# Queries one pair ahead, shared products in the last step, and a pair's rows turned a step later

## The chip, the cores and the metric

The kernel runs on one core of a Trainium2 chip. The metric is the device time of one execution in microseconds; for the kernel before, the median of three runs.

## The reference, cut to what matters

A decoder layer in fp32 over 1024 tokens (16 sequences of 64) of width 512. Each of three parts is added to its own input: an attention over the batch, a cross attention with 8 key heads of 4 query heads each, and a layer of experts. The change lies at the seam of the last two.

```
q = rmsnorm(layernorm(x) @ Wq.T);  p = softmax(q k.T / sqrt(128) + mask)
x = x + layernorm(x) + (p v) @ Wo.T          # 8 heads, summed over heads
h = layernorm(x)
scores = sigmoid(h @ gate.T) + bias;  top 4 of 16 experts, weights normed
x = x + h + sum_e w_e * Wd_e(silu(Wg_e h) * (Wu_e h)) + Sd(silu(Sg h) * (Su h))
```

## The kernel before, in words

The 1024 tokens are eight tiles of 128, taken in four **pairs** u = 0 to 3. The cross attention is a list of **steps** (g, u), head g = 0 to 7 and pair u. `cross` walks heads 4 and 5 in order, then heads 6 and 7 in turn, so that its last eight steps are (6,0), (7,0), (6,1), (7,1), ... (6,3), (7,3). A pair is complete once head 7 has run for it.

A step issues these pieces:

- `softmaxed` (L490): for both tiles, `normed_queries` scales the queries (L479), turns them (L482) and copies them to `qt` (L484, ScalarE); 64-column score products (L499); then on VectorE scale and mask (L504), maximum (L509), subtraction (L510), the exponential on ScalarE (L511), sum (L513), reciprocal (L514), product (L515).
- `queries` (L446): the query projection of a pair to come, seven products of two matmuls each (a Strassen-like scheme; `seven`, L254), evacuated on VectorE (L458 to L462) and squared on ScalarE (L466); their root (L442) is taken for one or more pairs at once.
- `projected` (L545): the output projection of the step before, again 14 matmuls, added into `acc` and `more` (L552, L557 to L559).
- `attended` (L518): the probabilities are turned (L521) and copied to `pt` (L525, ScalarE), multiplied by the values (L531), copied to `at` (L537, ScalarE), and combined to `sat` and `at` by four VectorE operations (L228 to L231) for heads 6 and 7.

After a pair is complete, `summed` (L571) combines the parts of its projection, and `normed_pair` (L622) takes the layer norm, writes the rows `xm` (L632), turns them with TensorE (L635), copies them to `xnT` (L636), and sends them to memory on SP's queue (L637). `routed_pair` (L689) multiplies them by the gate (L694), ranks the experts by comparing all with all (L710 to L714), counts (L722, L723), and leaves slots and weights; for pairs 0 to 2 `entered` (L776) scatters them to tables in memory with eight indirect DMAs from GpSimd. After the last pair, the tables are read on SP's queue (L793), added on GpSimd (L796 to L799), and joined with what the last pair adds by 8 matmuls (L771). Some small products make the lists of rows and experts for each block; `steer` (L898, L899) holds the expert of each block. Then SP issues the loads of expert weights (L926, three DMAs of 512 KB for a block that starts a new expert), and GpSimd gathers rows (L935). A block is turned (L943), multiplied by gate and up weights (L951) and by down weights (L971), and scattered into the output (L976).

Between the last pair's routing and the experts TensorE has the shared expert: `shared_half(0)` and `shared_half(1)`, each 16 matmuls of 512 columns (L825), a silu (L831), a product on VectorE (L832, `sz`), 8 matmuls (L839) and their addition to `acc` (L844).

What decides the order: the tile framework orders each engine's instructions when the program is built, by its own estimate of when each could start; each engine then runs its list in that order and waits where an operand is not there. PSUM is dealt out in three rings of banks: `mm` (3), `tr` (2) and `sc` (3).

Of the kernel before, what the change touches and what calls it, by code (L numbers as in the profile page):

```python
# [23 lines left out]
F32 = mybir.dt.float32  # L24
I32 = mybir.dt.int32
AF = mybir.ActivationFunctionType
ALU = mybir.AluOpType
# [21 lines left out]
def decoder_layer(  # L49
# [521 lines left out]
    def summed(u):  # L571
        x_sum, u3, c1, c2 = sums_of(u)
        V.tensor_add(x_sum[:, 1], x_sum[:, 0], x_sum[:, 1])
# [8 lines left out]

    def cross(steps):
        for g, u in steps:
# [4 lines left out]
            pr = softmaxed(g, u)  # L589
            if g < KVH - 2:  # L590
                queries(*divmod(NT // 2 * g + u + 3, NT // 2))
            elif g == KVH - 2:
                queries(g + 1, u)
            if (g, u) == (KVH - 3, NT // 2 - 1):
                queries(g + 1, u)
            if late:
                projected(*late.pop())
            late.append((g, u, *attended(g, u, pr)))
            if g == KVH - 2 and u > 0:
                summed(u - 1)  # L600
# [21 lines left out]
    def normed_pair(u):  # L622
# [5 lines left out]
        rs = inverse_root(mv[:, :, 1], [P, 2], 1.0)  # L628
        for j in range(2):
# [7 lines left out]
            nc.sync.dma_start(rows_d[i * P : (i + 1) * P, :], xm)  # L637
# [51 lines left out]
    def routed_pair(u):  # L689
# [15 lines left out]
        for j in range(2):  # L705
            other = sc[:, j, :].unsqueeze(1).to_broadcast([P, E, E])
            own = sc[:, j, :].unsqueeze(2).to_broadcast([P, E, E])
            gt = route.tile([P, E, E], F32, tag="gt", name="gt", bufs=1)
            eq = route.tile([P, E, E], F32, tag="eq", name="eq", bufs=1)
            V.tensor_tensor(gt, other, own, ALU.is_gt)  # L710
            V.tensor_tensor(eq, other, own, ALU.is_equal)
            V.tensor_mul(eq, eq, before_sb)
            V.tensor_add(gt, gt, eq)
            V.tensor_reduce(rank[:, j, :], gt, AX.X, ALU.add)  # L714
# [132 lines left out]
    def shared_half(th, queue):  # L847
        z = shared_hidden(th)
        for j in range(4):
            shared_out(th, z, j, queue)  # L850
# [228 lines left out]
```

## Time and profile before

| | us |
|---|---|
| median of 3 runs (1032.02 to 1035.42) | 1033.96 |
| the profiled execution | 1035.67 |
| its span, first to last instruction | 1033.7 |
| TensorE busy in the span | 979.8 |
| VectorE, ScalarE, GpSimd busy | 542.0, 435.3, 319.8 |
| first product of an expert block (L951) starts at | 800.5 |

The profile is of one execution. In its stretches, the steps (6,0) to (7,3) run from about 609 us to 748 us, the shared expert beside the last routing to 799 us, and the expert blocks to the end. Where rows of TensorE are shown, one fp32 matmul is two records of the profile, so "x8" is four matmuls. "PE" is TensorE, "DVE" VectorE, "ACT" ScalarE, "POOL" GpSimd, "SPq" the queue of SyncE. A bracket at the end of a row gives the idle time before it and what ended it. ScalarE loads a table of functions (`ACT_TABLE_LOAD`) when it goes from one kind of function to another (square root, exponential, silu).

### The profile page before, as it was taken

How to read it: one execution, taken by the hardware profiler on the slowest of the kernel's cores; microseconds unless marked ns; L12 is line 12 of the kernel's file. 1: busy time of each engine (PE TensorE's matmuls, PEld its weight loads, DVE VectorE, ACT ScalarE, POOL GpSimd, SP SyncE). 2: the span in 40 equal slices, each digit the busy share in tenths (PEclk: the TensorE clock that was granted, in tenths of full speed). 3: DMA queues.
4: the chain of work that ended last, by engine and by line, in shares of the span. 5: the costliest groups of instructions: out<-in, count | busy, mean ns of one | idle time of the engine just before them, and what ended most of it. 6: DMA issues, size and time to landing. Idle time of an engine off the chain costs nothing.

```text
span 1033.7 us, 13575 instructions
## 1 busy us (share of the span) xinstructions
PE 979.8 (95%) x4560; PEld 686.7 (66%) x4560; DVE 542.0 (52%) x1156; ACT 435.3 (42%) x1151; POOL 319.8 (31%) x318
## 2 busy tenths in 40 slices
PE   9999998999999999999999998988899999999974
PEld 3455556788888888887888887876654454545431
DVE  4566667574855747557557577768674111111100
ACT  2366663764545544535455554343220222222220
POOL 2131111512523417134252350033044343434332
PEclk9999999999999999999999999999799999999997
DMA  9120024200202002021020110001035856764643
GB/s 250 48 92 21 11 53 102 82 1 1 82 2 79 3 1 82 1 92 41 1 83 1 42 41 1 21 22 42 1 92 220 309 126 142 155 144 79 158 113 55
DMA packets 28362, 74.70 MB, mean 72 GB/s; under 512 B 4544, under 2 KB 8944, under 8 KB 26240
## 3 DMA queue, kind: packets, MB, share of 16 engines
q1 hardware_dynamic: 17728, 51.39, 15.0%
q0 software_dynamic: 10272, 22.13, 10.8%
q8 instruction: 38, 0.62, 0.3%
q14 instruction: 36, 0.29, 0.1%
q10 hardware_dynamic: 288, 0.26, 0.1%
HBM read 98.64 MB, written 14.97 MB: 110 GB/s over the span
## 4 chain that ended last, share of the span: by engine, by line
PE 76%; DVE 9%; ACT 5%; DMA 4%; issue 3%; POOL 1%; SPq 0%; ACTq 0%; POOLq 0%; DVEq 0%
PE mm L254 26%; PE sc L951 11%; PE sc L499 6%; PE mm L971 5%; PE sc L254 4%; PE sc L531 3%; PE mm L270 3%; PE tr L482 3%; PE sc L825 2%; PE mm L297 2%; DMA out_dram<-y,idx 2%; PE tr L297 2%; ACT square L466 2%; PE tr L943 1%; PE mm L839 1%
## 5 line engine op out<-in xcount | busy, mean ns | idle before, releaser
L951 PE MATMUL sc<-w,xt 128*128 128x512 f32 x288 | 131.4, 600 | 1.2 <-ACT xt L945 1.1
L466 ACT ACTIVATE square<-qraw 128x128 f32<-128x128 f32 x256 | 79.2, 309 | 74.7 <-DVE qraw L460 37.0
L976 POOL DMA_INDIRECT out_dram<-y,idx x36 | 56.8, 1578 | 120.5 <-DMA out_dram<-y,idx 82.6
L951 PEld LDWEIGHTS sc<-w,xt 128*128 128x128 f32 x288 | 52.6, 193 | 55.1 <-issue 53.2
L228 POOL TENSOR_TENSOR sat<-at 128x256 f32<-128x256 f32 x24 | 19.8, 823 | 209.9 <-ACT at L537 209.8
L956 DVE TENSOR_TENSOR z<-sc,z 128x256 f32<-128x256 f32 x36 | 15.3, 424 | 131.1 <-ACT z L955 131.1
L254 PE MATMUL mm<-wo_sb,at 128*128 128x256 f32 x256 | 70.5, 403 | 5.4 <-ACT at L537 5.4
L499 PEld LDWEIGHTS sc<-kT,qt 128*128 128x128 f32 x512 | 61.7, 191 | 18.0 <-ACT qt L484 9.9
L254 PE MATMUL mm<-wq_t,xns 128*128 128x256 f32 x256 | 70.5, 385 | 2.9 <-POOL wq_t L236 1.8
L971 PE MATMUL mm<-w,zt 128*128 128x512 f32 x144 | 68.2, 596 | 2.6 <-DVE zt L964 2.1
L254 PE MATMUL mm<-wq_sb,xnT 128*128 128x256 f32 x256 | 70.4, 381 | 0.0
L499 PE MATMUL sc<-kT,qt 128*128 128x64 f32 x512 | 69.1, 280 | 0.1
L254 PE MATMUL mm<-wo_t,sat 128*128 128x256 f32 x256 | 67.4, 383 | 0.6 <-DVE sat L229 0.6
L504 DVE SCALAR_TENSOR_TENSOR prob<-sc,mask_sb 128x512 f32<-128x512 f32 x32 | 22.0, 688 | 80.4 <-PE sc L499 80.4
L479 DVE TENSOR_TENSOR qraw<-qraw,rs 128x512 f32<-128x512 f32 x64 | 63.5, 1029 | 0.6
L782 POOL DMA_INDIRECT table_d<-entry_sb,at_slot x24 | 26.0, 1085 | 112.3 <-DVE at_slot L749 105.9
L254 PEld LDWEIGHTS mm<-wo_sb,at 128*128 128x128 f32 x256 | 50.9, 202 | 14.4 <-ACT at L537 7.2
L955 ACT ACTIVATE z<-sc 128x256 f32<-128x256 f32 x36 | 13.8, 384 | 108.4 <-PE sc L951 105.5
L254 PEld LDWEIGHTS mm<-wo_t,sat 128*128 128x128 f32 x256 | 48.6, 193 | 7.4 <-POOL wo_t L237 0.7
L254 PEld LDWEIGHTS mm<-wq_t,xns 128*128 128x128 f32 x256 | 46.8, 190 | 8.7 <-POOL wq_t L236 2.0
L971 PEld LDWEIGHTS mm<-w,zt 128*128 128x128 f32 x144 | 26.9, 190 | 35.8 <-issue 32.0
L484 ACT ACTIVATE qt<-tr,qw_sb 128x512 f32<-128x512 f32 x64 | 43.6, 689 | 16.5 <-PE tr L482 16.5
(272 smaller groups left out, 2039.4 us busy)
## 6 DMA issues: line engine op xcount, KB each, us to landing
w<-in_wg_dram SPq DMA_DIRECT2D x38, 512.0 KB
w<-in_wu_dram SPq DMA_DIRECT2D x38, 512.0 KB
w<-in_wd_dram SPq DMA_DIRECT2D x38, 512.0 KB
wq_sb<-in_wq_dram SPq DMA_DIRECT2D x8, 1024.0 KB
wo_sb<-in_wo_dram SPq DMA_DIRECT2D x8, 1024.0 KB
xs<-in_x_dram SPq DMA_DIRECT2D x8, 256.0 KB
wv_sb<-in_wv_dram SPq DMA_DIRECT2D x2, 1024.0 KB
ct<-in_ctxt_dram SPq DMA_DIRECT2D x8, 256.0 KB
```

The source lines that it names most:

```text
L254: T.matmul(dst, left[:, k, :], right[:, k, :], start=k == 0, stop=k == 1)
L270: T.matmul(kp, ctx_tiles[i][:, d, :], wk_sb[:, d, h * 512 : (h + 1) * 512], start=(d == 0), stop=(d == DC - 1),)
L297: T.matmul(vp, ctx_tiles[i][:, d, :], wv_sb[:, d, h * 512 : (h + 1) * 512], start=(d == 0), stop=(d == DC - 1),)
L466: S.activation(square, raw[:, h, :], AF.Square, accum_out=q_ss[g][:, 2 * u + j, h : h + 1])
L479: V.tensor_mul(raw, raw, q_rs[g, i // 2][:, i % 2, :].unsqueeze(2).to_broadcast([P, GRP, HD]))
L482: T.transpose(tp[:, j * P : (j + 1) * P], raw[:, j, :], ident)
L484: S.activation(qt.rearrange("p b h q -> p h b q"), tp.rearrange("p (h b q) -> p h b q", h=GRP, b=2), AF.Copy, scale=qw_sb,)
L499: T.matmul(sp[:, at : at + C], qt[:, b, 2 * hp : 2 * hp + 2, :], kT[g // 4][:, g % 4, k0 : k0 + C], start=True, stop=True,)
L531: T.matmul(pv[b][:, j * 256 : (j + 1) * 256], v[g // 4][rows, 2 * u + j, g % 4 * HD : (g % 4 + 1) * HD], pt[rows, j, :], start=True, stop= ...
L951: T.matmul(hp, xt[:, d, :], w1_tiles[buffer(j)][:, :, d, :], start=(d == 0), stop=(d == DC - 1))
L971: T.matmul(op, zt[:, c, :], w2_tiles[buffer(j)][:, c, :], start=(c == 0), stop=(c == FI // P - 1))
L976: G.indirect_dma_start(out, bass.IndirectOffsetOnAxis(idx[:, b : b + 1], axis=0), y, None, bounds_check=NT * P - 1, oob_is_err=False, comp ...
```

## The change

Five edits, all around the last eight steps.

1. Head 7's queries are issued in other steps: those of pair 0 in (6,0), and those of pair u+1 in (7,u). Before, (6,u) issued those of pair u.
2. A complete pair is combined and normed in head 7's next step, behind that step's softmax: `summed` now takes a multiplier `mark`, which is computed from the finished probabilities and is always 1. `normed_pair` writes its rows by ScalarE (scale and bias) in place of VectorE, sends them to memory, and returns them.
3. The turn of those rows and the copy to `xnT` are a function of their own, `pair_turned`, called a step later, in (6,2), (6,3) and, for pair 2, in (7,3); the routing follows at the end of the same step. For pairs 0 to 2 the turn uses the `mm` ring.
4. The ranking compares both tiles of a pair in one set of operations; the two counting products of each tile change places.
5. The first eight shared matmuls (with their silu and product) are issued in (7,3), in the `mm` ring.

```diff
-    def summed(u):
+    def summed(u, one=1.0):
         x_sum, u3, c1, c2 = sums_of(u)
-        V.tensor_add(x_sum[:, 1], x_sum[:, 0], x_sum[:, 1])
+        V.scalar_tensor_tensor(x_sum[:, 1], x_sum[:, 0], one, x_sum[:, 1], ALU.mult, ALU.add)
...
+    routed = {(KVH - 2, 2): 0, (KVH - 2, 3): 1, (KVH - 1, 3): 2}
+    rows = {}
...
             pr = softmaxed(g, u)
+            if g == KVH - 1 and u > 0:
+                mark = small.tile([P, 1], F32, tag="mark", name="mark", bufs=1)
+                V.tensor_tensor(mark, pr[:, 0, 0:1], pr[:, 0, 0:1], ALU.is_equal)
+                summed(u - 1, mark)
+                rows[u - 1] = normed_pair(u - 1)
             if g < KVH - 2:
                 queries(*divmod(NT // 2 * g + u + 3, NT // 2))
-            elif g == KVH - 2:
+            if (g, u) in ((KVH - 3, NT // 2 - 1), (KVH - 2, 0)):
                 queries(g + 1, u)
-            if (g, u) == (KVH - 3, NT // 2 - 1):
-                queries(g + 1, u)
+            pair = routed.get((g, u))
             if late:
                 projected(*late.pop())
+            if pair is not None and g == KVH - 2:
+                pair_turned(pair)
+            if g == KVH - 1:
+                if u + 1 < NT // 2:
+                    queries(g, u + 1)
+                else:
+                    shared_hidden(0, 0, mm_bank)
             late.append((g, u, *attended(g, u, pr)))
-            if g == KVH - 2 and u > 0:
-                summed(u - 1)
-                normed_pair(u - 1)
-                if u > 1:
-                    entered(u - 2, 1)
-            if g == KVH - 1 and u > 0:
-                routed_pair(u - 1)
-                entered(u - 1, 0)
+            if pair is not None:
+                if g == KVH - 1:
+                    pair_turned(pair)
+                routed_pair(pair)
+                if pair > 0:
+                    entered(pair - 1, 1)
+                entered(pair, 0)
...
-            V.tensor_scalar(xm, acc[:, i, :], mv[:, j, 0:1], rs[:, j : j + 1], ALU.subtract, ALU.mult)
-            tp = tr_bank()
+            S.activation(xm, acc[:, i, :], AF.Identity, bias=off[:, j : j + 1], scale=rs[:, j : j + 1])
+            nc.sync.dma_start(rows_d[i * P : (i + 1) * P, :], xm)
+            xms.append(xm)
+        return xms
+
+    def pair_turned(u):
+        for j, xm in enumerate(rows.pop(u)):
+            i = 2 * u + j
+            tp = mm_bank() if u < NT // 2 - 1 else tr_bank()
             for d in range(DC):
                 T.transpose(tp[:, d * P : (d + 1) * P], xm[:, d * P : (d + 1) * P], ident)
             S.copy(xnT[:, :, i * P : (i + 1) * P], tp.rearrange("p (d t) -> p d t", d=DC))
-            nc.sync.dma_start(rows_d[i * P : (i + 1) * P, :], xm)
...
-        for j in range(2):
-            other = sc[:, j, :].unsqueeze(1).to_broadcast([P, E, E])
...
+        other = sc.unsqueeze(2).to_broadcast([P, 2, E, E])
+        own = sc.unsqueeze(3).to_broadcast([P, 2, E, E])
...
+        V.tensor_tensor(gt, other, own, ALU.is_gt)
+        V.tensor_tensor(eq, other, own, ALU.is_equal)
+        V.tensor_mul(eq, eq, before_sb.unsqueeze(1).to_broadcast([P, 2, E, E]))
+        V.tensor_add(gt, gt, eq)
+        V.tensor_reduce(rank, gt, AX.X, ALU.add)
...
-            T.matmul(pp[:, j, :], ones_sb, taken[:, i, :], start=True, stop=False)
-            T.matmul(pp[:, j, :], tri_sb, sel[:, j, :], start=False, stop=True)
+            T.matmul(pp[:, j, :], tri_sb, sel[:, j, :], start=True, stop=False)
+            T.matmul(pp[:, j, :], ones_sb, taken[:, i, :], start=False, stop=True)
...
     def shared_half(th, queue):
-        z = shared_hidden(th)
+        for ic in range(th == 0, FI // P):
+            shared_hidden(th, ic, sc_bank)
...
     projected(*late.pop())
     summed(NT // 2 - 1)
-    normed_pair(NT // 2 - 1)
+    rows[NT // 2 - 1] = normed_pair(NT // 2 - 1)
+    pair_turned(NT // 2 - 1)
```

`shared_hidden` now does one of its two halves a call, with the banks given to it. In the order of the built program, the row writes of the last pair stand between the reads of the tables on SP's queue, with the first of the four output rows of `shared_half(0)` among them; before, all eight reads came first. In the last step the product of the shared half (L856 of the changed file, as L832 here) stands on VectorE between the subtraction (L510) and the sum (L513) of the last softmax.

More of the change, by code (lines that the diff above doesn't have):

```diff
@@ L628, in normed_pair @@
         rs = inverse_root(mv[:, :, 1], [P, 2], 1.0)
+        off = small.tile([P, 2], F32, tag="off", name="off", bufs=1)
+        V.scalar_tensor_tensor(off, mv[:, :, 0], -1.0, rs, ALU.mult, ALU.mult)
+        xms = []
         for j in range(2):
@@ L704, in routed_pair @@
         rank = route.tile([P, 2, E], F32, tag="rank", name="rank", bufs=2)
-        for j in range(2):
-            other = sc[:, j, :].unsqueeze(1).to_broadcast([P, E, E])
[L707 to L714, printed above, removed]
+        other = sc.unsqueeze(2).to_broadcast([P, 2, E, E])
+        own = sc.unsqueeze(3).to_broadcast([P, 2, E, E])
+        gt = route.tile([P, 2, E, E], F32, tag="gt", name="gt", bufs=1)
+        eq = route.tile([P, 2, E, E], F32, tag="eq", name="eq", bufs=1)
+        V.tensor_tensor(gt, other, own, ALU.is_gt)
[3 more added lines that the diff above has]
+        V.tensor_reduce(rank, gt, AX.X, ALU.add)
         sel = route.tile([P, 2, E], F32, tag="sel", name="sel", bufs=2)
@@ L816, in load_shared, with shared_hidden @@
         shared_w[part + 1] = sw
-    def shared_hidden(th):
-        z = shared.tile([P, FI // P, 512], F32, tag="sz", name="sz", bufs=1)
+    shared_z = {}
+    def shared_hidden(th, ic, new_bank):
+        if ic == 0:
+            shared_z[th] = shared.tile([P, FI // P, 512], F32, tag="sz", name="sz", bufs=1)
         sw1 = shared_w[1]
-        for ic in range(FI // P):
-            ps = [sc_bank() for _ in range(2)]
-            for s in range(2):
-                for d in range(DC):
-                    T.matmul(
-                        ps[s], sw1[:, s, d, ic * P : (ic + 1) * P],
-                        xnT[:, d, th * 512 : (th + 1) * 512],
-                        start=(d == 0), stop=(d == DC - 1),
-                    )
-            si = shared.tile([P, 512], F32, tag="ssi", name="ssi", bufs=2)
-            S.activation(si, ps[0], AF.Silu)
-            V.tensor_mul(z[:, ic, :], ps[1], si)
-        return z
+        ps = [new_bank() for _ in range(2)]
+        for s in range(2):
+            for d in range(DC):
+                T.matmul(
+                    ps[s], sw1[:, s, d, ic * P : (ic + 1) * P],
+                    xnT[:, d, th * 512 : (th + 1) * 512],
+                    start=(d == 0), stop=(d == DC - 1),
+                )
+        si = shared.tile([P, 512], F32, tag="ssi", name="ssi", bufs=1)
+        S.activation(si, ps[0], AF.Silu)
+        V.tensor_mul(shared_z[th][:, ic, :], ps[1], si)
     def shared_out(th, z, j, queue):
@@ L847, in shared_half @@
     def shared_half(th, queue):
-        z = shared_hidden(th)
+        for ic in range(th == 0, FI // P):
+            shared_hidden(th, ic, sc_bank)
         for j in range(4):
-            shared_out(th, z, j, queue)
+            shared_out(th, shared_z[th], j, queue)
     cross([(g, u) for g in range(KVH // 2, KVH - 2) for u in range(NT // 2)])
```

## The prediction

> **What bounds the kernel now.** I read the page first. TensorE is busy 95% of the span, so a gain can only come from where it waits or is clocked down.
>
> ```profile
> span 1033.7 us, 13575 instructions
> PE 979.8 (95%) x4560; PEld 686.7 (66%) x4560; DVE 542.0 (52%) x1156; ACT 435.3 (42%) x1151; POOL 319.8 (31%) x318
> PEclk9999999999999999999999999999799999999997
> ```
>
> One slice of the clock row shows 7 (723.6 to 749.4 us): the last step of the last two heads. Next the windows by stage, where the columns are the window, its length, then busy time of TensorE, weight load, VectorE, ScalarE, GpSimd, and the granted clock. From 800 us on (routed experts) TensorE is full; from 640 to 749 us, where the change works, it is not.
>
> ```profile
> 640.00:660.00 20.00, 18.18 (x109) 15.46 (x109) 13.60 (x29) 8.00 (x16) 0.00 (x0) 1.00 0.07 27
> 660.00:697.00 37.00, 32.62 (x189) 27.55 (x189) 28.59 (x79) 14.81 (x36) 9.20 (x8) 0.95 0.05 15
> 697.00:734.00 37.00, 28.66 (x163) 23.89 (x162) 27.62 (x77) 13.75 (x31) 8.52 (x8) 0.90 0.09 29
> 734.00:749.00 15.00, 14.33 (x57) 11.58 (x57) 10.61 (x41) 2.56 (x4) 0.25 (x1) 0.69 0.01 1
> 800.00:860.00 60.00, 59.72 (x186) 29.59 (x185) 8.53 (x21) 15.80 (x31) 25.11 (x21) 1.00 0.72 212
> ```
>
> Then TensorE's timeline; the bracket is the wait and what ended it.
>
> ```profile
> 642.95 1.99 PE L254 MATMUL mm<-wo_sb,at 128*128 128x256 f32 x8 [1.16 <-ACT at L537]
> ...
> 673.17 1.13 PE L254 MATMUL mm<-wo_t,at 128*128 128x256 f32 x4 [1.89 <-DVE qraw L462]
> 676.31 1.13 PE L531 MATMUL sc<-pt,v 64*128 64x256 f32 x8 [0.71 <-ACT pt L525]
> 678.88 3.47 PE L254 MATMUL mm<-wo_sb,at 128*128 128x256 f32 x8 [1.44 <-ACT at L537]
> ...
> 731.70 1.09 PE L521 MATMUL tr<-ident,prob 128*128 128x128 f32 x4 [3.96 <-DVE prob L515]
> 732.58 3.43 PE L694 MATMUL tr<-gate_sb,xnT 128*128 128x16 f32 x16
> ```
>
> Three waits in a row (1.89 for the evacuation of queries, 0.71, 1.44) come in step (head 6, pair 2), again at 710 to 716 us, and one of 3.96 for the last softmax. After each the same products take nearly double: 3.47 us at 678.88 against 1.99 at 642.95. From 639 to 748 us the waits sum to 15.2 us (0.68+1.16+0.35+1.89+0.71+1.44+0.35+1.88+0.71+1.44+3.96+0.67). The slow clock costs 1.5 us here, 1.7 at 716, and 5.4 from 731.7 to 743.5 (1.09 for 0.60, 3.43 for 1.86 and so on, each against the same group in an earlier step): 8.5 us in all. So 24 us is the ceiling.
>
> Last, the road from the last routing to the experts, and the loads' share of the DMA (window 806 to 810 us).
>
> ```profile
> 758.55 1.85 PE L694 MATMUL tr<-gate_sb,xnT 128*128 128x16 f32 x16
> 783.53 0.17 DVE L899 CAST steer<-fresh 1x48 int32<-1x48 f32 x1
> 785.53 0.37 SPq L926 DMA_DIRECT2D w<-in_wg_dram  x1
> 800.46 3.70 PE L951 MATMUL sc<-w,xt 128*128 128x512 f32 x8 [0.28 <-ACT xt L945]
> q1 hardware_dynamic: 247, 0.93, 56.8%
> ```
>
> Gate products end at 760.4, `steer` at 783.7, the first expert's products start at 800.5. TensorE fills these 40 us with shared products (37 of the 48 of 0.86 us), so nothing waits. Summing the load queue's bytes in windows of 4 us, gate and up weights of blocks 0 to 3 are in at about 790.6, 797.9, 805.5 and 811.4, while their products start at 800.5, 804.6, 810.6 and 816.4. The least slack is 5.0 us: the experts can start no sooner than steer + 11.8 us (800.5 - 783.7 - 5.0), whatever TensorE does. That bound is hidden today.
>
> **The change, part by part.** Steps are (head, pair), heads 0 to 7. The order of instructions in the two built programs is the same on TensorE until the queries of (7,1), at 621.6 us.
>
> *Queries one pair ahead.* The 14 products (0.43 us each, 6.0 us), the copy, the 8 squares with their read-outs (0.43 us each) and the 5 VectorE combines are the same, only placed as one block ahead of an L521 instead of around it. This removes the 1.89 and 1.88 us waits and the drops behind them (1.5 + 1.7): 7.0 us. It also takes away the products that lay between L521 and the next L254. And five or more squares now stand in ScalarE's queue ahead of the `at` copies (L537): in (7,1) the order has a square, `pt`, a square, `qt`, two `xm` writes, a square, then `at`. With 0.43, 0.6, 0.43, 0.7, 1.3 and 0.43 us, `at` is ready about 1.7 us after TensorE asks for it. Queued behind it are all 14 output products of that pair.
>
> *Pair combined behind the softmax.* `mark` ties L573 to L515. Six VectorE operations (some 3.5 us: 0.34+0.34+0.6+0.6, two BN stats 0.6 each) no longer precede the softmax, but now precede `sat` (L228). In the last step this costs TensorE about 1.2 us beyond the 1.1 us wait for `at`.
>
> *Rows written by ScalarE.* Two tensor-scalars of 0.54 us leave VectorE. An Identity with pointer scale and bias is not in the trace; nearest are L511 (0.63) and L484 (0.69, pointer scale). I take 0.65 each, between 0.6 and 0.7; counted above. Their two row writes on SP stay in step order; around the last pair four table reads and one output row now mix with them, and each is ready within 2 us of its turn: nothing, or 2 us if the reads land late (they have some 7 us before L775 needs them).
>
> *Turn a step later.* Eight transposes (0.9 us) move between the pair's last product and L521, where VectorE finishes the softmax: they fill 0.9 us. But the `xnT` copies (2 x 0.5 us) then precede `pt`, and the gate products wait for them: 0.3 us, and 1.1 us for `at` after, in (6,2) and (6,3). In (6,3) the exponential waits for five squares and a table load: L521 about 1.6 us late.
>
> *Merged rank.* Five operations of 512 columns (0.6 us pitch as L557) for ten of 256 (0.34): 3.0 for 3.4 us. Swapped tri/ones: nothing, two products of 0.22 us.
>
> *Table loads.* ScalarE's order has 16 from this point on where it had 10. The trace shows 1.28 us each with the next instruction directly behind (713.40 + 1.28, then L442 at 714.70). The Trainium skill (ScalarE: Activation LUTs, What ACT_TABLE_LOAD costs) adds a drain and speaks of about 2.66 us per switch. By the row the six add 7.7 us to an engine that is 40% busy, and about 1.3 us of it is on a path, in (6,3). By the page it would be 16 us, with 4 more on the path. I take the row.
>
> *Shared products in the last step.* Eight products of 0.86 us (6.9 us) fill the hole before L521 of (7,3). But VectorE's order puts their product (L856) ahead of the softmax's sum (L513), and L856 waits for the eighth. So L513, L514 and L515 start when TensorE runs dry: 0.65+0.65+0.2+0.7 = 2.2 us of wait remain of 3.96. Then 0.7 (`pt`), 1.1 (`at`) and 1.2 (`sat`).
>
> *The tail.* Pair 2's routing (some 6.5 us of VectorE) now lies after L521 of (7,3), ahead of pair 3's BN stats and of the second L856, and TensorE runs out before that: about 2.6 us.
>
> **Sum.** Waits after: 1.5 (6,1), 2.2 (7,1), 2.1 (6,2), 0.3 (7,2), 2.8 (6,3), 5.4 (7,3), 2.6 tail = 16.9 us. I take 15.0, since durations added in this way leave out some 3.6 us of switching between kinds of products (against today's steps), and half of that falls into waits. So as much waiting as now. Work from 621.6 us to the last gate product is now 138.8 - 16.2 (0.9 more before 639) - 8.5 = 114.1 us. After, it loses 11 shared products (9.5), and gains 16 plus 8 output products (20.6): 125.3 us.
>
> For the clock there is a rule against a row. The Trainium skill (TensorE: Matmul & The Clock Gate, HAM oscillation) lets the clock drop when a gap exceeds a free-running window of some 3.4 us[...]. But 1.89 + 0.71 + 1.44 us with short products between did drop it (granted 0.62 and 0.52 from 678 to 682). By the rule the last step, with no wait above 2.3 us, loses nothing; by the row its 5.4 us of waits within 7 us lose one or two windows. I take the row, 3.5 us (0 to 6.3).
>
> Last gate product: 621.6 + 125.3 + 15.0 + 3.5 = 765.4. From there to `steer` 20.4 us: today's 23.3, less four L844 in between (0.6 us each), less 0.4 for the merge. Steer 785.8. TensorE would be through its filler (24 shared products 20.6, table products 5, a turn 0.9) at 765.4 + 26.6 = 792, but the weights allow 785.8 + 11.8 = 797.6. Against 800.5 that is 2.9 us. The profiled execution (1035.67) would be 1032.8; on the median of 1033.96, 1.7 lower, **1031.1 us**. Of some 14 us of shared products taken forward, the load bound and the later gate keep back most.
>
> **The rivals.**
> *The clock holds* (0.25): last gate 761.9, steer 781.3 (19.4 us, if GpSimd's table adds miss the chain), experts 793.1, 7.4 us gained: 1026.6, down to 1022 if weights come sooner. For: the page's rule, and fillers before the last step. Against: the drop at 678.
> *It does not do what it says* (0.10): TensorE already runs queries of (7,1) ahead of L521 of (7,0), so "one pair ahead" may only trade one wait for another: 1034.
> *Slower* (0.23): the last pair's road decides. The clock stays low through the mixed gate products as from 730 to 743 us (6.3 us), all 16.9 us of waits stand, and GpSimd's four table adds (now 759.8 to 768) fall on the rank chain; beside them operations took 1.49 for 0.42 us: 3 us on the 19.4. Gate 770.1, steer 792.5, experts 804.3, so 3.8 us later: 1037.8. It loses from a steer later than 788.7.
> *As summed* (0.42): 1028 to 1034.
>
> A difference of 0.3% (3.1 us) is what a measurement can tell. Faster: 0.25 and nearly half of the last case, 0.44. Same: 0.31. Slower: 0.25. The range runs from well into the first rival to just past the slower one, 1023 to 1039.
>
> **What would show it.** Right: no wait on qraw L462; in (7,3) L521 waits 2 to 2.5 us behind L856; `steer` at 784 to 788; products of block 2 or 3 waiting for a DMA of `w`. Wrong: full clock throughout; experts dense from 792; or a pair's `at` more than 2.5 us late.

## The result and the profile after

The changed kernel takes 1053.18 us (median of 6 runs, 1046.15 to 1054.5), the kernel before beside it 1033.17 (1028.0 to 1036.81). The recorded ratio of the two is 1.0158, with a 95% interval of 1.0127 to 1.019 (the medians by themselves are 1.9% apart): 1.6% slower, where 0.3% faster was forecast, and outside the range. The profiled execution took 1053.17 us, its span is 1051.4.

The page first (span, busy time, granted clock in 40 slices):

```profile
span 1051.4 us, 13570 instructions
PE 989.4 (94%) x4560; PEld 692.0 (66%) x4560; DVE 538.3 (51%) x1135; ACT 447.5 (43%) x1165; POOL 317.5 (30%) x318
PEclk9999999999999999999999999888898999999997
```

TensorE does the same 4560 records as before and is busy 9.6 us longer; the rest of the 17.7 us of span is idle time. Apart from the last slice, one slice of the clock row was low before, now it is five. The windows by stage say where:

```profile
660.00:697.00 37.00, 33.64 (x189) 28.20 (x187) 24.86 (x69) 14.58 (x38) 7.74 (x8) 0.91 0.08 18
697.00:734.00 37.00, 32.26 (x162) 26.23 (x161) 22.86 (x62) 18.15 (x35) 2.31 (x3) 0.82 0.15 27
734.00:749.00 15.00, 9.21 (x28) 5.00 (x27) 9.61 (x23) 6.39 (x9) 6.37 (x6) 0.73 0.01 1
800.00:860.00 60.00, 55.38 (x164) 27.14 (x165) 11.02 (x33) 11.80 (x23) 26.88 (x27) 0.97 0.81 269
```

The clock fell from 0.95 to 0.91 and from 0.90 to 0.82 in the first two rows, and the experts (last row), which were dense with 59.72 us, now have holes. TensorE's timeline shows what stands in front of each slow stretch:

```profile
678.00 3.78 PE L254 MATMUL mm<-wo_sb,at 128*128 128x256 f32 x8 [1.15 <-ACT at L537]
...
699.38 1.51 PE L531 MATMUL sc<-pt,v 64*128 64x256 f32 x8 [1.91 <-ACT pt L525]
...
720.29 3.77 PE L254 MATMUL mm<-wo_sb,at 128*128 128x256 f32 x8 [1.16 <-ACT at L537]
...
741.27 1.09 PE L521 MATMUL tr<-ident,prob 128*128 128x128 f32 x4 [2.50 <-DVE prob L515]
...
747.72 2.04 PE L254 MATMUL sc<-wo_sb,at 128*128 128x256 f32 x4 [2.56 <-DVE at L231]
```

The wait on qraw is gone, and the wait behind L856 is 2.50 us, both as forecast. But eight output products take 3.78 and 3.77 us, against 1.99 at full clock. Up to the last gate product no single wait is longer than 2.6 us, and four steps, (6,2), (7,2), (6,3) and (7,3), lose the clock: 2.8 us of slow products from 676.5, 3.5 from 700, 2.7 from 717 and 3.3 from 741, each against the same group in an undisturbed step, 12.4 us together. Before it was 8.5. Laid out in windows of 0.1 us, the granted clock is at half from 676.1 to 683.0, 700.0 to 706.8, 717.1 to 723.9 and 741.0 to 751.2 us. Those are stretches of 3.4 us, two or three in a row, and each costs up to 1.7 us.

Last, the road to the experts, in order: TensorE, ScalarE, VectorE, TensorE again, as far as the first products of the experts (L976) and beyond.

```profile
774.43 1.90 PE L717 MATMUL tr<-gate_sb,xnT 128*128 128x16 f32 x16
```
```profile
775.23 1.28 ACT L723 ACT_TABLE_LOAD   x1
779.35 0.20 ACT L723 ACTIVATE rsc<-tr 128x32 f32<-128x32 f32 x1 [2.84 <-remote]
```
```profile
784.23 0.69 DVE L738 TENSOR_SCALAR sel<-rank 128x32 f32<-128x32 f32 x1
785.06 1.25 DVE L748 TENSOR_TENSOR cw<-sel,rsc 128x32 f32<-128x32 f32 x1
786.37 0.73 DVE L743 TENSOR_TENSOR taken<-taken,sel 128x16 f32<-128x16 f32 x1
...
790.01 0.34 DVE L790 TENSOR_SCALAR at_row<-iota_sb,row,by 128x128 f32<-128x128 f32 x1
...
802.26 0.17 DVE L924 CAST steer<-fresh 1x48 int32<-1x48 f32 x1
```
```profile
785.07 0.36 PE L744 MATMUL tr<-sel,tri_sb 128*128 128x16 f32 x2 [2.63 <-DVE oh L759]
...
786.51 6.49 PE L849 MATMUL sc<-xnT,sw 128*128 128x512 f32 x8
792.83 0.59 PE L793 MATMUL tr<-at_row,at_col 128*128 128x256 f32 x2
...
812.41 0.92 PE L968 MATMUL tr<-ident,xg 128*128 128x128 f32 x4 [2.73 <-DMA xg<-rows_d,idx]
813.12 5.07 PE L976 MATMUL sc<-w,xt 128*128 128x512 f32 x8
...
825.45 3.67 PE L976 MATMUL sc<-w,xt 128*128 128x512 f32 x8 [0.80 <-DMA w<-in_wu_dram]
```

The last gate products end at 776.3, `steer` is written at 802.4, the first expert's products start at 813.1. ScalarE takes up `rsc` 3.0 us after the gate products end. Three small operations take 2.67 us where undisturbed ones take 0.17 or 0.18 each: they lie beside GpSimd's table additions (783.62 to 787.1), and each ends within 0.05 us of the end of one of these. The kernel before has the same, with about the same loss, 2.1 us:

```profile
764.48 1.49 DVE L712 TENSOR_TENSOR eq<-eq,before_sb 128x256 f32<-128x256 f32 x1
765.89 1.28 DVE L737 TENSOR_TENSOR oh<-rank,choice_sb 128x64 f32<-128x64 f32 x1
```

TensorE, which had waited 2.63 us for the ranking, goes through a fifth slow stretch (half clock from 785.4 to 792.2 us): four shared products take 6.49 us, where 3.7 are usual. The first table product (L793) stands behind them and starts 2.5 us after its operands are written (790.35); before, it was 0.5 us. Then TensorE waits for gathered rows and for weights, and the first products of the experts run in a sixth slow stretch, 5.07 us for 3.70.

### The profile page after: what moved, and what is told of

Same layout as the page of the kernel before. It is cut to its first block, busy times and chain, and to the rows that moved or that the text cites. A ratio compares the mean times of both kernels' runs of the same rounds, so it can differ in the third digit from the quotient of the medians.

```text
span 1051.4 us, 13570 instructions
## 1 busy us (share of the span) xinstructions
PE 989.4 (94%) x4560; PEld 692.0 (66%) x4560; DVE 538.3 (51%) x1135; ACT 447.5 (43%) x1165; POOL 317.5 (30%) x318
## 3 DMA queue, kind: packets, MB, share of 16 engines
q0 software_dynamic: 10272, 22.13, 10.7%
## 5 line engine op out<-in xcount | busy, mean ns | idle before, releaser
L976 PE MATMUL sc<-w,xt 128*128 128x512 f32 x288 | 133.2, 607 | 2.6 <-DMA w<-in_wu_dram 1.9
L976 PEld LDWEIGHTS sc<-w,xt 128*128 128x128 f32 x288 | 53.5, 196 | 57.7 <-issue 56.6
```

Of the source, the lines that this page charges most:

```text
L976: T.matmul(hp, xt[:, d, :], w1_tiles[buffer(j)][:, :, d, :], start=(d == 0), stop=(d == DC - 1))
```

## The experiments

Theory 1 says that the regrouping leaves TensorE several short waits a step, and that the slow clock behind them carries the loss. Rival 1: the later turn and the shared products do, not the queries. Rival 2: shared products ahead of the last gate delay `steer` one for one. Rival 3: the clock does not hang on the waits. Rival 4: ScalarE's row writes.

Every run lists its span and mean granted clock. So each kernel's loss can be split: **short of full clock** is span times (1 - mean clock), **full-clock part** is the span less that (means over a kernel's runs). The first is not all loss, since idle time counts too. But it moves with the time: over 70 runs of the kernel before on chip A the correlation is 0.83 with 0.89 us of span per us, and in 21 of 24 sets of runs it is above 0.7. This shows that the two go together, not which causes which. All times are against the kernel before on the same chip, where it was 17.7 to 18.5 us short, with 1014.4 to 1016.3 us at full clock.

| kernel | chip | ratio (95%) | short of full clock, us: change | full-clock part, us: change |
|---|---|---|---|---|
| after | first | 1.0158 (1.0127 to 1.019) | +12.0 | +4.7 |
| after | B | 1.0075 (1.0043 to 1.0108) | +5.2 | +4.2 |
| after | C | 1.0127 (1.0108 to 1.0145) | +8.3 | +6.5 |
| after | D | 1.0073 (1.0047 to 1.0099) | +3.8 | +3.8 |
| before, queries ahead | A | 1.0038 (1.0019 to 1.0058) | +0.6 | +3.0 |
| before, shared products early | B | 1.0018 (0.9995 to 1.0042) | -2.1 | +3.3 |
| after, queries and shared products undone | C | 1.0026 (0.9999 to 1.0053) | +3.5 | -0.1 |
| after, shared products undone | A | 1.0075 (1.0051 to 1.01) | +8.5 | +0.1 |
| the same, waits filled | C | 1.0036 (1.0012 to 1.0059) | -3.4 | +7.4 |
| after, rows on VectorE | B | 1.001 (0.9986 to 1.0033) | -0.1 | +2.7 |
| the same, two steps filled | C | 1.0031 (1.001 to 1.0052) | -1.2 | +4.5 |
| after, order mended | C | 1.0131 (1.0113 to 1.0148) | +10.1 | +2.6 |
| after, three steps filled | A | 1.0021 (1.0 to 1.0042) | -3.8 | +6.1 |
| after, last step filled | D | 1.0053 (1.0028 to 1.0078) | -0.8 | +6.2 |
| after, two steps filled | D | 1.0094 (1.0062 to 1.0126) | +3.7 | +5.2 |
| after, load held | D | 1.009 (1.0062 to 1.0119) | +4.8 | +3.7 |
| before, filled | A | 0.9963 (0.9941 to 0.9985) | -2.1 | -1.2 |
| before, more filled | C | 0.9957 (0.9933 to 0.998) | -4.7 | +0.1 |
| before, shared early and filled | B | 0.9981 (0.9952 to 1.0009) | -1.3 | +1.9 |

(For the first row the kernel before is its one profiled run. The ratio comes from the times and the two parts are means, so they need not add up to the last tenth of a per cent; the rows of 4 and 5 runs, "after, order mended" and "after" on C, differ most.)

### One part alone

**Queries one pair ahead, in the kernel before.**

```diff
-            elif g == KVH - 2:
-                queries(g + 1, u)
-            if (g, u) == (KVH - 3, NT // 2 - 1):
+            if (g, u) in ((KVH - 3, NT // 2 - 1), (KVH - 2, 0)):
                 queries(g + 1, u)
             if late:
                 projected(*late.pop())
+            if g == KVH - 1 and u + 1 < NT // 2:
+                queries(g, u + 1)
```

> The kernel before with one edit of the change: head 7's queries one pair ahead (those of pair 0 in (6,0), of pair u+1 in (7,u), ahead of the values product). Turn, routing, rows and shared products stay as before. Theory 1 (regrouping the products leaves TensorE short waits behind L521, and these bring the clock down): the two waits of 1.9 us on qraw go, but waits for at of 1.2 us and more come, with slow stretches behind them; 1031 to 1038 us, no gain. Rival 1 (the later turn and routing and the shared products are at fault): the 7.0 us of waits and slow clock go and nothing comes, so 1028 us, held there by the weight loads.

Measured 1.0038, 1037.71 us: the time that theory 1 expected, but not by its cause. The qraw waits go and others come; from 609 us to the last gate products the waits sum to 20.2 us, against 17.0 before. Rival 1's gain of 5 us is not there. The loss is 3.0 us at full clock, and only 0.6 us of it is clock.

**Shared products early, in the kernel before.** `shared_hidden` and `shared_half` as in the kernel after, and `shared_hidden(0, 0, mm_bank)` ahead of `attended` in (7,3).

> The kernel before with only the edit of the shared products: the first eight are issued in (7,3). In this build they stand before L521 of (7,3), and the VectorE product of their silu stands behind the softmax's last product, not ahead of its sum. Theory 1 (what the clock and the waits lose is what counts): the 4.0 us hole before L521 is filled and the slow stretch from 731 to 743 us goes, so steer comes 2 to 3 us sooner although 6.9 us more stand before it, and fewer shared products are left behind it; 1026 to 1030 us. Rival 2 (shared products ahead of the last gate delay steer one for one, and the weight loads do not let the experts start sooner): 1034 to 1040 us.

Measured 1.0018 (1037.28 us), not told apart from no change, and within rival 2's span. The clock gains 2.1 us and the full-clock part loses 3.3. The profiled run has the last gate at 762.7 (760.4 before), `steer` at 786.7 and the experts at 797.5: they start 10.7 us behind `steer`, where the kernel before has 16.8, and then take 4.5 us longer to the end. So 6.9 us of shared products taken forward, 4.0 of which lay in a hole, delayed `steer` by 3.0 us, and the 3.0 us by which the experts started sooner were lost behind their start.

**What is left: rows, turn and ranking.** The kernel after with `queries(g + 1, u)` back in (6,u) and the shared products behind the last pair.

> The kernel after with head 7's queries in their old steps and the shared products behind the last pair: what is left of the change is the combining behind the softmax, rows on ScalarE, the turn a step later and the merged ranking. If the parts simply add (1.58% in all, 0.38% for the queries, 0.18% for the shared products), 1043 to 1045 us. Theory 1: here too the gate products follow L521 with a wait for at behind them, with slow stretches, 1038 to 1045 us. If the loss comes only from the parts together: 1033 to 1036 us.

Measured 1.0026 (1039.85 us), within theory 1's span, though the interval just reaches no change; the clock loses 3.5 us, the full-clock part nothing. The parts alone sum to 0.8%, which is what the kernel after shows on chips B and D, and half to two thirds of it on the other two.

**After without the shared products in the last step.**

```diff
-                else:
-                    shared_hidden(0, 0, mm_bank)
...
-        for ic in range(th == 0, FI // P):
+        for ic in range(FI // P):
```

> The kernel after, with the eight shared products of the last step put back behind the last pair (the sixteen stand together again, in the sc ring). Theory 1 (clock after short waits): the 2.5 us wait behind the shared product's VectorE step goes, but a hole of some 4 us comes back before L521 of (7,3); the clock loss in (6,2), (7,2), (6,3) stays: 1049 to 1055 us. Rival 2 (the shared products in the last step cost the time, by the last softmax and by missing in the tail): 1043 to 1047 us, and first experts to end is 233 us again, not 238.

Measured 1041.77 us, below both spans, and first experts to end is 233.0 us again. The full-clock part is that of the kernel before (1014.5 us against 1014.4 on the chip); all that is lost, 8.5 us, is clock. With the run on the shared products alone: at full clock these cost 3 to 4 us, and the rest of the change together costs nothing there (the 3.0 us of the queries alone do not come back here, where they are included). Every kernel with the shared products split, this one too, also has one buffer for the result of the silu in place of two, which the list of the change leaves out; here it costs nothing that the full-clock part shows.

### Filling the waits

**Three steps of the kernel after.** Transposes of the identity into a bank that the real ones overwrite, or that has been read:

```diff
-        tp = tr_bank()
+        tp = tr_bank(); [T.transpose(tp[:, :P], ident, ident) for _ in range({(6, 3): 6, (7, 3): 8}.get((g, u), 0))]
...
-        quarters = [at[:, 2 * k : 2 * k + 2, :] for k in range(4)]
+        [T.transpose(tp[:, :P], ident, ident) for _ in range({(6, 2): 5, (6, 3): 5, (7, 3): 12}.get((g, u), 0))]; quarters = [at[:, 2 * k : 2 * k + 2, :] for k in range(4)]
```

> The kernel after, with 36 extra transposes of the identity on TensorE (0.22 us each, 7.8 us in all, results overwritten or never read) in the waits: 5 behind L531 in (6,2), 6 before L521 and 5 behind L531 in (6,3), 8 before L521 and 12 behind L531 in (7,3). The order of all other instructions is unchanged on TensorE, VectorE and ScalarE. Theory 1: these waits are filled, the clock stays full there, and the last gate product comes about 8 us sooner (768 against 776.3): 1044 to 1048 us although work is added. Rival 3 (the clock does not hang on the waits, but on the slow products themselves): no gain, 1052 to 1056 us, and the eight products behind at still take 3.8 us.

Measured 1035.69 us, lower still than theory 1 said: with work added, the kernel takes less than in any of its own four measurements. Its timeline, to be held against the rows at 678.00, 720.29, 747.72 and 774.43 above:

```profile
678.87 1.99 PE L254 MATMUL mm<-wo_sb,at 128*128 128x256 f32 x8
...
713.09 1.99 PE L254 MATMUL mm<-wo_sb,at 128*128 128x256 f32 x8 [0.46 <-ACT at L537]
...
738.22 1.10 PE L254 MATMUL sc<-wo_sb,at 128*128 128x256 f32 x4 [0.52 <-DVE at L231]
...
763.20 1.90 PE L717 MATMUL tr<-gate_sb,xnT 128*128 128x16 f32 x16
```

The products take 1.99 us, and the last gate ends at 765.1, 11.2 us sooner. Three single stretches of half clock are left, 3.4 us each. The full-clock part (+6.1) is within those of the kernel after; the clock is 7.6 to 15.8 us better than in its four measurements. This kernel was run on another chip than any of those, which is why the next runs share one. Its sibling without the shared products, unfilled, ran on chip A too and lost 8.5 us of clock there.

**One chip, step by step.** First the kernel after itself; then the same two lines with {(7, 3): 8} and {(7, 3): 12}; then with {(6, 3): 6} and {(6, 2): 5, (6, 3): 5}.

> The kernel after, as the measure on this chip for the three runs beside it. The two earlier measurements of these instructions gave 1.58% and 1.27% above the kernel before, and the run whose load was meant to move (its build had the same instruction order on all engines) 0.75%. Expected here: 0.7 to 1.6% above the kernel before, 1042 to 1053 us.

> The kernel after with extra transposes of the identity in (7,3) alone: 8 before L521 and 12 behind L531 (4.3 us of work in 5.8 us of waits). Theory 1: the slow stretch from 741 us goes, last gate product 5 to 7 us sooner, the end 5 to 8 us below the kernel after on this chip. Rival 3 (the clock does not hang on the waits): within 2 us of it.

> The kernel after with extra transposes in (6,2) and (6,3) alone: 5 behind L531 in each, 6 before L521 of (6,3) (3.5 us of work in 4.0 us of waits). Theory 1: the slow stretches at 678 and 717 us go (2.8 and 2.7 us), the end 4 to 7 us below the kernel after on this chip, and together with the run on (7,3) this makes up the gain of filling all three. Rival 3: within 2 us of it.

Measured 1.0073, 1.0053 and 1.0094. The last step's filler brings the clock back by 4.6 us but costs 2.4 us at full clock: 2.2 us less span, under what was expected. By the times both runs lie within 2 us of the kernel after and their intervals overlap with its own, which is what rival 3 said; only the clock part of the first speaks for theory 1. The filler in the two steps brings nothing, against theory 1 as I put it. Its timeline shows one place where the clock went:

```profile
707.91 0.82 PE L519 MATMUL tr<-ident 128*128 128x128 f32 x6
709.75 0.66 PE L521 MATMUL tr<-ident,prob 128*128 128x128 f32 x4 [1.02 <-DVE prob L515]
710.25 2.20 PE L717 MATMUL tr<-gate_sb,xnT 128*128 128x16 f32 x16
712.37 2.08 PE L531 MATMUL sc<-pt,v 64*128 64x256 f32 x8
714.38 1.33 PE L538 MATMUL tr<-ident 128*128 128x128 f32 x5
715.61 3.37 PE L254 MATMUL mm<-wo_sb,at 128*128 128x256 f32 x8
```

The granted clock is 0.50 from 711.8 to 715.2 us: it is lost behind a wait of 1.02 us, in the 16-column gate products, before the wait that the last filler covers. L531 has 2.08 us for 1.14, and the output products are slow without any wait ahead of them. With the same instructions up to here, the kernel with three steps filled kept the clock (1.86 for the gate, 1.14 for L531), and in the profiled run of the kernel after on this chip L531 of this step (1.14) and the output products behind it (1.99) kept it as well, in spite of a wait of 1.16 us between them. So a given wait doesn't decide it. Over all the runs with fillers, the clock part fell by 2.1 to 11.9 us in the five where the last step was filled (against the same kernel unfilled; for the kernel after, against its best measurement); the three with (6,2) and (6,3) alone, here and below, moved it by 1.1 us at most. Four of the five filled the other steps as well, so this points to the last step but doesn't prove it.

**After without shared products, filled.** The same lines with {(6, 3): 6, (7, 3): 18} and {(6, 2): 5, (6, 3): 5, (7, 3): 12}.

> The kernel after without shared products in the last step (as in the run on that, whose mean granted clock left it 26 us short of full clock over its span, against 18 us for the kernel before), with extra transposes of the identity in its waits: 5 behind L531 in (6,2) and (6,3), 6 before L521 of (6,3), 18 before L521 and 12 behind L531 of (7,3), 9.9 us of work in some 11 us of waits; the order within the last step changes with it. Theory 1: at full clock this kernel is as long as the kernel before, and the whole of its 0.75% was the clock, so with the waits filled it comes to 0.995 to 1.001 of the kernel before, with 14 to 17 us short of full clock. Rival 3 (fillers do not bring the clock back): 1.007 to 1.012.

Measured 1.0036 (1041.05 us), above theory 1's span and below rival 3's. The clock came back as theory 1 said, 15.1 us short in place of 26.2; the time did not, because the full-clock part rose by 7.3 us (each against the kernel before on its chip). The scheduler changed the last step: shared products stand ahead of the gate products again, the experts start 11.6 us behind `steer` and take 242.3 us to the end.

**The kernel before, filled.** {(7, 3): 12} with {(6, 2): 6, (6, 3): 6, (7, 3): 3}, and then {(7, 3): 16} with {(6, 2): 8, (6, 3): 8, (7, 3): 6}.

> The kernel before with 27 such extra transposes: 6 behind L531 in (6,2) and in (6,3), 12 before L521 and 3 behind L531 in (7,3), 5.8 us of added work in 7.5 us of waits. Theory 1: the slow stretches at 678, 716 and in part at 731 go, the last gate product comes 5 to 7 us sooner, and the end 3 to 5 us sooner (the weight loads then hold the experts): 1028 to 1030 us. Rival 3: 1033 to 1038 us.

> The kernel before with more extra transposes than in the run that had 27: 8 behind L531 in (6,2) and in (6,3), 16 before L521 and 6 behind L531 of (7,3), 8.2 us of work in 7.5 us of waits. Theory 1: what was left of slow clock at 735 us goes as well, 0.993 to 0.996 of the kernel before; the weight loads end the gain there. If the added work outruns the waits: 0.997 to 1.000.

Measured 0.9963 and 0.9957 (1030.73 and 1032.02 us, beside 1034.54 and 1036.43): 0.4% faster than the kernel before, with useless work in waits and nothing else changed. The clock row of the second has no low slice but the last:

```profile
PEclk9999999999999999999999999999999999999998
```

**Shared products early and fillers, in the kernel before.** The edit of the shared products with {(6, 2): 6, (6, 3): 6} behind L531.

> The kernel before with the shared products in (7,3) as in the run above, and six extra transposes of the identity behind L531 in (6,2) and in (6,3). Theory 1: the slow stretches at 678 and 716 us go too, 3 us more than the run above: 1023 to 1027 us, below the kernel before and the kernel after. Rival 2: no better than the kernel before, 1033 to 1038 us.

Measured 0.9981 (1036.22 us): no better than the kernel before, as rival 2 said, and not told apart from it. The 0.4% against shared products alone is within the two intervals, and it stands in the full-clock part (1.9 us for 3.3), not in the clock (1.3 us gained for 2.1): fillers in (6,2) and (6,3) brought no clock here either.

### ScalarE

**Rows on VectorE, in the kernel after,** and then with {(6, 2): 5, (6, 3): 5} behind L531:

```diff
-            S.activation(xm, acc[:, i, :], AF.Identity, bias=off[:, j : j + 1], scale=rs[:, j : j + 1])
+            V.tensor_scalar(xm, acc[:, i, :], mv[:, j, 0:1], rs[:, j : j + 1], ALU.subtract, ALU.mult)
```

> The kernel after with the rows xm written by VectorE (tensor-scalar, as before) in place of ScalarE; in this build the order within the last step changes too, all eight shared products stand before L521 and the gate products of pair 2 behind it. Rival 4 (the two 0.75 us row writes and table loads on ScalarE make the copies to at late, and through this the clock drops): the wait for at in (7,1) falls from 1.2 to 0.4 us, the slow stretch at 700 us goes, 1040 to 1046 us. Theory 1 with the holes of (6,2) and (6,3) untouched: 1047 to 1053 us.

> The kernel after with the rows on VectorE, and five extra transposes of the identity behind L531 in (6,2) and in (6,3); all other instructions keep their order. Theory 1: the waits for at (1.2 us each) are filled, the slow stretches at 678 and 716 us go, and the end comes 3 to 5 us sooner than with the rows on VectorE alone (1038.3 us): 1033 to 1036 us. Rival 3 (the clock does not hang on these waits): 1038 to 1041 us.

Measured 1.001 (1038.32 us) and 1.0031 (1040.28 us). The first is 0.65% below the kernel after on its chip (that is the run with the load, below), a little less than the 7 to 13 us that rival 4 said. The wait for `at` in (7,1) is 0.23 us, as it expected. But from L521 of (6,1) to L521 of (7,3) the two profiled runs take the same time, 94.6 and 94.3 us, and from there to the last gate product 27.6 and 35.2 us: the gain comes in the last step, whose order the edit changed.

```profile
730.90 7.03 PE L849 MATMUL mm<-xnT,sw 128*128 128x512 f32 x16
737.76 0.60 PE L521 MATMUL tr<-ident,prob 128*128 128x128 f32 x4
```

All eight shared products stand together and L521 follows without a wait; behind it the waits are 0.73 and 1.35 us at full clock, where the kernel after has 0.73 and 2.56 us and the slow clock. The second is 0.96% below the kernel after on its own chip, C. Since the two ran on different chips, and the second has both of ScalarE's delays (below), they don't show whether the fillers gave anything.

**Order mended, rows still on ScalarE.** In (7,3) `one` is `mark`, elsewhere 1.0:

```diff
-        V.tensor_mul(shared_z[th][:, ic, :], ps[1], si)
+        V.scalar_tensor_tensor(shared_z[th][:, ic, :], ps[1], one, si, ALU.mult, ALU.mult)
```

> The kernel after with one dependence added: the product of the first shared silu (L856) is multiplied by mark as well, so that on VectorE it stands behind the last softmax's product (L515) and not ahead of its sum (L513). Order on TensorE is as in the kernel after but for two products, on ScalarE it is the same. Theory 1 (short waits and the slow clock behind them; the rows on ScalarE only matter through this order): the 2.5 us wait of L521 in (7,3) goes, and in part the slow stretch from 741 us; last gate product 3 to 6 us sooner, 1046 to 1050 us. Rival 4 (writing the rows on ScalarE is itself the cost): 1052 to 1055 us.

Measured 1.0131 (1049.57 us), on the chip where the kernel after has 1.0127 (1050.49 us): nothing gained. The mend works in its place (L521 waits 0.97 us, not 2.50), the full-clock part is 3.9 us less than that of the kernel after, and the clock part 1.8 us more. The ratio speaks for rival 4, but by the means 2.1 us are gained, and these are 4 runs against 5. Whether the row writes or the order on TensorE carry the gain of the run before stays open.

**The down weights' load.** In the kernel after ScalarE took up `pt` of (7,2) 1.7 us after L521 ended, just behind this load. The first edit moves `load_shared(1)` from (6,3) to (7,3); the second makes the load wait for the last softmax as well (`G.tensor_copy(sw[:, 0, 0:1], after)` ahead of it).

> The kernel after with the load of the shared down weights (512 KB) issued one step later, at the end of (7,3) and not of (6,3). In the kernel after this load was issued at 694.95 us, and ScalarE then began the copy to pt of (7,2) 1.3 us after its operand was there; the clock fell to half behind it, 1.9 us of wait and 3.5 us of slow products. If the load causes this: the wait at L531 of (7,2) is 0.2 to 0.4 us, full clock at 700 to 707, 1047 to 1049 us. If it was chance or another cause: as the kernel after, 1051 to 1055 us.

> The kernel after with the load of the shared down weights held back until the last softmax: GpSimd writes one column of its tile from the probabilities of (7,3) first, and the load stands two row writes later on SP's queue; order on the other three engines unchanged. If this load is what makes ScalarE late at pt of (7,2): the 1.7 us from L521's end to pt goes wherever the kernel after shows it, with the slow clock behind it, 4 to 6 us. If not: within 2 us of the kernel after on this chip, and the delay at pt still there if it is there in the kernel after.

The first did not do what it was to: the scheduler put the load in the old place, at 693.95 us, so this is the kernel after, on chip B. It took 1044.78 us, and neither ScalarE delay was in it. The second moved the load to 734.91 us and took 1.009, against 1.0073 beside it, and again neither kernel showed the delay. So the load is not shown to be the cause, nor cleared: on these two chips there was no delay to take away.

**The kernel after, on chip C.**

> The kernel after once more, for more times beside these runs and a second profile. If ScalarE's late pt in (7,2) (1.9 us of wait, 3.5 us of slow clock) and its 2.8 us of idle time ahead of the last rsc belong to the kernel, both are seen again and the time is 1050 to 1055 us. If they were chance, one or both are missing, and runs spread down to 1040 us.

Measured 1.0127 (1050.49 us), and both delays came again to a hundredth. ScalarE's `pt` and `rsc`, in the kernel after on the first chip, the same on C, and on D:

```profile
698.75 0.58 ACT L525 COPY pt<-tr 128x512 f32<-128x512 f32 x1 [2.04 <-PE tr L482]
```
```profile
701.55 0.58 ACT L525 COPY pt<-tr 128x512 f32<-128x512 f32 x1 [2.05 <-PE tr L482]
...
782.16 0.20 ACT L723 ACTIVATE rsc<-tr 128x32 f32<-128x32 f32 x1 [2.85 <-remote]
```
```profile
696.24 0.59 ACT L525 COPY pt<-tr 128x512 f32<-128x512 f32 x1 [0.37 <-PE tr L521]
...
768.33 0.20 ACT L723 ACTIVATE rsc<-tr 128x32 f32<-128x32 f32 x1
```

The first chip and C are also the two where the kernel after loses most. The other profiles say more. On C, `pt` of (7,2) is late by 1.7 us with the order mended and with the rows on VectorE and filled as well, and the last `rsc` by 3.0 and 3.3 us in these two. With queries and shared products undone only `rsc` is late, by 1.7 us. In the eight profiles of changed kernels on A, B and D both come within 0.2 us, and so they do without shared products, filled, on C. The rows on VectorE have the delays on C and not on B, with the same order but for ten added transposes. So the delays go with the chip or the time of the runs, and not with the order alone; what makes them is open.

## Why the prediction was wrong, step by step

| step | forecast | measured (profiled run) |
|---|---|---|
| no wait on qraw | yes | yes |
| waits (6,1) to the tail | 16.9, taken as 15.0 | 16.8 |
| L521 of (7,3) behind L856 | 2.2 | 2.5 |
| **slow clock up to the last gate** | **3.5** (0 to 6.3) | **12.4** |
| last gate product | 765.4 | 776.3 |
| gate to `steer` | 20.4 | 26.1 |
| `steer` to experts | 11.8 at least | 10.7 |
| first expert to end | 233.2, as before | 238.3 |

**The step that failed is the clock:** 3.5 us was forecast, 12.4 measured. I saw that waits of 1.89 + 0.71 + 1.44 us had dropped it, and took that row and not the Trainium skill's rule against gaps longer than some 3.4 us (TensorE: Matmul & The Clock Gate, HAM oscillation); with shorter gaps taken as safe, which was my reading of it, the term would have been nothing. That choice was right: no wait up to the last gate exceeds 2.6 us. But I then charged the row to the last step alone. My own list of waits had the same pattern in (6,2) and (6,3): a wait for the softmax, 16-column gate products in place of full ones, and a wait for `at`. The fourth place, (7,2), was not on it: I had 0.3 us of wait there, and ScalarE's late `pt` made 1.9. So the consequence was priced in one place of four: 8.9 us of the 10.9 by which the last gate is late. Of what remains, waits give 1.8 us and a start of the stretch 1.2 us later the rest, with 1.0 the other way. In all four measurements of the kernel after the clock term goes up, by 3.8 to 12.0 us, where I had it fall by 5.0.

The four profiles of the kernel after agree on this. Time lost to the clock in each, as (1 - granted clock) times time in windows of 1 us, whether TensorE worked or waited in it:

| profile | (6,2) | (7,2) | (6,3) | (7,3) | behind the last gate |
|---|---|---|---|---|---|
| before | 1.7 | 0 | 1.7 | 6.8 | 0 |
| after, first chip | 3.4 | 3.4 | 3.4 | 5.1 | 5.1 |
| after, C | 3.4 | 3.4 | 3.4 | 5.1 | 5.1 |
| after, B | 3.4 | 0 | 3.4 | 5.1 | 5.1 |
| after, D | 3.4 | 0 | 0 | 5.0 | 1.7 |

Step (6,2) loses as much in each, (6,3) in three of four, and (7,2) only where `pt` was late. The loss comes in units of 1.7 us, a stretch of 3.4 us at half clock. In the last step the kernel before had lost more, so what I had as the worst place was the one that improved.

**The waits** came out right in their sum (16.8 us for 16.9) by luck. The tail has 0.2 us where I had 2.6, (7,2) has 1.9 for 0.3, and 0.6 us fell in (7,0), which I had left out; the other five are within 0.7 us of the list. Of my four signs of being right three were seen (no qraw wait, 2.5 us behind L856, a block waiting for `w`: 0.80 us at 825.45); the fourth, `steer` at 784 to 788, was not (802.4). One sign of being wrong was met as well, barely: in (7,3) the last wait for `at` is 2.56 us. The table loads cost what the row said (702.00 + 1.28 us, the next instruction at 703.30).

**Gate to `steer`.** Of the 5.7 us too little, 3.0 are ScalarE's late `rsc`, which nothing in the profile of before hinted at. Another 2.0 are the clock again: the wait for the late ranking is followed by the fifth slow stretch, and the table product stands behind it. On B and D, where `rsc` came at once, TensorE did not wait there and this stretch is missing; gate to `steer` took 23.9 us on B, with half as long a stretch later, and 21.9 on D. The rest is one L844 (0.6 us) that did not come off the chain. VectorE beside GpSimd's additions is not part of the error: it loses 2.15 us now, but 2.1 us of the same were in the 23.3 us from which I started.

**The load bound** did not quite hold: the experts start 10.7 us behind `steer`, 1.1 us sooner than the 11.8 that I had as the least (on C 9.9 us). It is near enough to show that they start as soon as they can. But I took experts that start at the bound to run densely from there, as when the weights had 16.8 us of lead. They don't: in the kernel after they take 5.1 us longer, with waits for gathered rows and weights, and 1.4 us of slow clock in the first products. So taking filler forward ends in a loss, not in a smaller gain, as the shared products alone show (+3.3 us at full clock).

**The sum** of the errors is 10.9 + 5.7 - 1.1 + 5.1 = 20.6 us, which is the whole distance from the forecast span (1030.8) to 1051.4. ScalarE's delays, with the waits and slow stretches behind them, are some 10 us of it (an estimate from the profile: 1.6 + 3.5 + 3.0 + 2.0). Without them, on B and D, the kernel is still 0.7% slower than the one before. The slower rival named these mechanisms (clock low, all waits stand, the additions on the chain, late `steer`), but its clock of 6.3 us was half of what came, and its `steer` at 792.5 was 9.9 us early.

**What is shown and what is not.** Shown: the loss has a clock part and a full-clock part on every chip; with the waits of three steps filled the clock part is gone (on chip A, where the kernel after itself did not run), and the same remedy makes the kernel before faster; without the early shared products, and without fillers, the full-clock part is gone (0.1 us up or down in two kernels). Not shown: which wait takes the clock in a given run, since filling (6,2) and (6,3) alone changed nothing, and why clock came back only where the last step was among those filled; the cause of ScalarE's two delays; how far the row writes matter apart from the order they bring about.

## What to carry to other kernels

When a change trades one long hole for several short ones, add up what TensorE does in each stretch of a few us, small products counted as little (how little is not measured here), and price the slow clock in every step that has the pattern, not only in the worst; then test by filling the holes with work that nobody needs. Work taken forward ahead of the instruction that starts the next phase's loads delays that phase, save for what of it lies in a hole: 6.9 us less a hole of 4.0 made 3.0 here. An edit that moves one instruction to another engine can reorder the whole step in a scheduled build: compare the built orders, and measure on more than one chip.

## What the runs showed of the hardware

The granted clock can fall to half behind a single wait of 1.02 us, in 16-column products (0.50 from 711.8 to 715.2 us in the run with two steps filled), and the same instructions may keep it in another run. In the profiles read here the half clock lasts 3.4 us or two, three or four times that (6.8, 10.2, 13.6). The times of one kernel spread by up to 15 us (1025.43 to 1040.69 for the kernel before on chip D), and time and mean clock go together, with correlations of 0.5 to 0.97 in size over the kernels. Small VectorE operations beside GpSimd additions (0.73 to 1.33 us each) took 0.69 to 1.49 us in place of 0.17 to 0.42. ScalarE started two instructions 1.7 and 3.0 us after their operands were there, by the same amounts in two profiled executions of the kernel after on two chips, and not in those on two others; some other kernels with the change showed it on one of the first two chips as well.
